# Four quads' rows of k and v loaded by SyncE instead of gathered by GpSimd, in a graph attention kernel

## The chip, the cores and the metric

The kernel runs on one core of one Trainium2 chip. A core has a matrix engine (TensorE, PE in the profile, with its weight loads as PEld), a vector engine (VectorE, DVE), a scalar engine (ScalarE, ACT), GpSimd (POOL) and SyncE (SP), which only starts transfers. SP and POOL each work off one queue of instructions in order. The transfers themselves run on 16 DMA engines. The metric is the time of one execution on the device in microseconds, the median of several runs.

## What is computed

There are 6250 nodes with 128 features each and 206250 edges, sorted by receiver. Each edge has two vectors of 32 features and a cutoff. With 8 heads of 16 features:

```python
w_ij = silu(edge_feats @ rad_W1 + rad_b1) @ rad_W2 + rad_b2
w_ij = w_ij + (silu(chi_scalar @ sph_W1 + sph_b1) @ sph_W2 + sph_b2)
q_i = (node_feats @ Wq)[receivers]          # all split into 8 heads of 16
k_j = (node_feats @ Wk)[senders]
alpha = (q_i * w_ij * k_j).sum(axis=-1) / sqrt(16) * cutoffs[:, None]
v_j = (node_feats @ Wv)[senders]
out = segment_sum(alpha[..., None] * v_j, receivers, num_segments=n_nodes) / 16
x = layernorm(x + out)
```

All is float32. What matters here: k and v belong to an edge's sender, and the senders are random nodes, so these rows have to be fetched one by one. The receivers are sorted, so q and the sums are local.

## The kernel before

**Tiles.** 128 edges make a tile, 4 tiles a quad (512 edges), 4 quads a group. There are 403 quads in 101 groups. Within a group the quads are worked in the order 0, 2, 1, 3; their places in this order are the slots 0 to 3, and `order` lists all quads in this way.

**Start.** The kernel multiplies all nodes by Wk and Wv and stores the result as a table `kv_tab` in device memory, one row of 256 numbers (1 KB) for each node: k first, then v. The senders lie in SBUF as `src_i`, one column for each tile and one partition for each edge of it.

**Loop.** For each quad, `hidden_of` (L371) puts the edge features through the first layers on PE, ACT applies silu (L396), `weigh` (L403, L405) does the second layers, `q_at_edges` (L378) brings q to the edges, `multiply` (L410) makes u = q * w on DVE, and `turn_back` (L416) turns u so that edges lie on partitions. For the quad before, `scores` (L421, L423, L424) multiplies by k and sums over each head, `messages` (L432) multiplies by v, and `sum_quads` (L442) adds messages up by receiver on PE. `statistics` (L475 to L491) makes the layernorm of a group's rows two groups later; every fourth time it writes four groups of rows.

**Rows of k and v.** `gathers(q)` issues four gathers on POOL (L114), one for each tile: each fetches 128 rows of `kv_tab` by a column of `src_i` into the tile `kv`, of which there are 16 (`RING`). They are issued 14 quads (`AHEAD`) before the quad is worked, so far as buffers and POOL allow. `kv_of[q]` names the tile that L421 and L432 read.

**Order.** All is recorded under a manual schedule: every engine works in the order in which the code names its instructions. A scheduler does not change it. So SP's queue in the loop is, for each group g: in slot 0, the load of x for g+2 (L156, with the place read from a table into a register, L118) and the load of relb (the receivers' places, as used for one-hot tables) for g+1 (L150); in slot 1, the load of edge features for g+2 (L141); in slot 2, where four groups are complete, four writes of output rows (L491, place from L118). Features and relb have two buffers each; the features' buffer is free when `hidden_of` has read the last quad of group g. DMAs from SP take turns over eight completion semaphores, and a DMA waits for the one eight before it. POOL's gathers have eight of their own.

A second, general path (L704 on) handles receivers for which the local sums don't suffice. With these inputs its loop runs zero times.

Of the kernel before, what the change touches and what calls it, by code (L numbers as in the profile page):

```python
# [13 lines left out]
F32 = mybir.dt.float32  # L14
# [7 lines left out]
SP = mybir.EngineType.SP  # L22

P = 128
N = 6250
D = 128
# [5 lines left out]
QT = 4  # L32
# [10 lines left out]
LB = 4  # L43
XQ = 8
RING = 16
CHECK = 20
NEIGHBORS = 16.0
EPS = 1e-5
# [3 lines left out]
@with_exitstack  # L52
def gnn_kernel(ctx, tc, x, src, dst, weight, edges, rad_W1, rad_b1, rad_W2, rad_b2,
               sph_W1, sph_b1, sph_W2, sph_b2, Wq, Wk, Wv, out):

# [8 lines left out]
    nc = tc.nc  # L66
# [3 lines left out]
    kv_tab = dram.tile([NB * P, 2 * D], F32, name="kv_tab")  # L70
# [6 lines left out]
    src_i = const.tile([P, NT], I32, name="src_i")  # L77
# [14 lines left out]
    gb_i = const.tile([1, NG], I32, name="gb_i")  # L92
# [17 lines left out]
    def quad_of(name, bufs, width=D):  # L110
        return ep.tile([P, QT, width], F32, name=name, bufs=bufs)
# [5 lines left out]
    def start_of(table, i, last):  # L117
        return nc.values_load(table[:1, i:i + 1], engines=(SP,), min_val=0, max_val=last,  # L118
                              skip_runtime_bounds_check_because="the table is clamped to it")
# [3 lines left out]
    order = [g * NQ + j for g in range(NG) for j in (0, 2, 1, 3) if g * NQ + j < QUADS]  # L123
    pairs = []
    for q in order:
        if q % NQ < 2:
            pairs.append([q])
        else:
            pairs[-1].append(q)
    feats_of, relb_of, act_of, kv_of, hot_of, hotT_of, x_of, q_of, msg_of = ({} for _ in range(9))  # L130
    po_of, part_of, to_of, tot_of, xT_of, y0_of, u_of, pick_of, pq_of = ({} for _ in range(9))

    def gathers(q):
        kv = quad_of("kv", RING, 2 * D)
        for t in range(QT):
            gather(kv[:, t, :], kv_tab, src_i[:, q * QT + t:q * QT + t + 1])
        kv_of[q] = kv

    def load_feats(g):
        feats_of[g] = gp.tile([P, EG // 2], F32, name="feats")  # L140
        nc.sync.dma_start(feats_of[g], edges[g])  # L141
# [4 lines left out]
    def load_rel(g):  # L146

        relb_of[g] = gp.tile([P, EQ], BF16, name="relb")
        r = rel_lin[g * GT:(g + 1) * GT, :].rearrange("(j t) e -> j (t e)", j=NQ)
        nc.sync.dma_start(relb_of[g], r[:, None, :].to_broadcast([NQ, W, EQ]))  # L150
# [180 lines left out]
    with tc.tile_pool(name="ps", bufs=1, space=PSUM) as pp:  # L331
        def pick(g):

            n = quads_in(g)
            pick_of[g] = gp.tile([P, NQ, W], F32, name="pick")
            nc.vector.tensor_tensor(
                pick_of[g][:, :n, :], colp[:, None, :W].to_broadcast([P, n, W]),
                off[:, g, :n, None].to_broadcast([P, n, W]), op=OP.is_equal)
# [110 lines left out]
        def place(g):  # L449

            to = to_of[g] = gp.tile([P, 2, P], F32, name="to")
            nc.vector.tensor_scalar(to[:, 0, :], colp, rowq[:, g:g + 1], None, op0=OP.is_equal)
            nc.vector.tensor_scalar(to[:, 1, :], colp, rowp[:, g:g + 1], None, op0=OP.is_equal)

        def part_sums(g):
            n = quads_in(g) * W
            part_of[g] = gp.tile([P, D], F32, name="part")
            nc.scalar.activation(part_of[g][:n, :], po_of[g][:n, :], AF.Copy)  # L458
# [10 lines left out]
        def statistics(g):  # L469
            first = g // LB * LB if g < NG - 2 else g  # L470
            if g == first:
                y0_of[g] = (gp.tile([P, LB, D], F32, name="y0"), gp.tile([P, LB, 2], F32, name="mv"))
            y0, mv = y0_of[first]
            k = g - first + 1
            nc.vector.tensor_tensor(y0[:, k - 1, :], tot_of[g], x_of[g], op=OP.add)  # L475
            st = gp.tile([P, 6], F32, name="st")
            nc.vector.bn_stats(st, y0[:, k - 1, :])
            nc.vector.bn_aggr(mv[:, k - 1, :], st)
            if k == LB or g >= NG - 3:
                sd = gp.tile([P, LB], F32, name="sd")  # L480
                nc.scalar.activation(sd[:, :k], mv[:, :k, 1], AF.Sqrt, bias=eps)
                rs = gp.tile([P, LB], F32, name="rs")
                nc.vector.reciprocal(rs[:, :k], sd[:, :k])
                shift = gp.tile([P, LB], F32, name="shift")
                nc.vector.scalar_tensor_tensor(shift[:, :k], mv[:, :k, 0], -1.0, rs[:, :k],
                                               op0=OP.mult, op1=OP.mult)
                for i in range(k):
                    nc.scalar.activation(y0[:, i, :], y0[:, i, :], AF.Identity,  # L488
                                         scale=rs[:, i:i + 1], bias=shift[:, i:i + 1])
                    r = start_of(gb_i, first + i, N - P)  # L490
                    nc.sync.dma_start(out[ds(r, P), :], y0[:, i, :])  # L491

        def outside(o, values, low, high):

# [13 lines left out]
        def verdict():  # L508
# [4 lines left out]
            nc.vector.tensor_reduce(found, pe[:1, :8], AX.X, OP.add)  # L513
            nc.vector.tensor_scalar(general, found, 0.0, None, op0=OP.is_gt)

        pick(0)
        turn_q(0)
        make_q(0)
# [7 lines left out]
        for g in range(NG):  # L526
            last = g == NG - 1
            for slot, j in enumerate((0, 2, 1, 3)):
                q = g * NQ + j
                i = g * NQ + slot  # L530
                if q >= QUADS:
                    continue
                if i + AHEAD < len(order):
                    gathers(order[i + AHEAD])
                if slot == 0 and 2 <= g:
                    part_sums(g - 2)
                    if g == CHECK + len(checks) + 1:
                        verdict()
                if before is not None:
                    pu = turn_back(before)  # L540
                w = weigh(q)
                if slot % 2 == 0:
                    u = 2 * g + slot // 2 + 1
                    q_and_hidden(pairs[u - 1], pairs[u] if u < len(pairs) else [])
                if slot == 1 and 2 <= g:
                    sum_group(g - 2)
                if slot == 1 and g + 1 < NG:
                    turn_q(g + 1)
                if slot == 3:
                    make_q(g + 1)  # L550
                if 1 <= g:
                    for t in ((), (0, 1), (2, 3))[slot] if last else ((), (0, 1), (2,), (3,))[slot]:
                        sum_quads(g - 1, t)
                if before is not None:
                    alpha = scores(before, pu)
                multiply(q, w)
                if before is not None:
                    messages(before, alpha)
                before = q
                if slot == 0:  # L560
                    if g + 2 < NG:
                        load_x(g + 2)
                    if g + 1 < NG:
                        pick(g + 1)
                        if 1 <= g:
                            load_rel(g + 1)
                if slot == 1:
                    if g + 2 < NG:
                        load_feats(g + 2)
                    if 1 <= g:  # L570
                        place(g - 1)
                    if last:
                        place(g)
                if slot == 2 and g + 1 < NG:
                    one_hots_T(g + 1)
                if slot == 2 and 2 <= g:
                    statistics(g - 2)
                if slot == 3:
                    one_hots(g + 1)
                    if CHECK <= g < CHECK + len(checks):  # L580
                        checks[g - CHECK]()
        g = NG - 1
# [6 lines left out]
        messages(before, scores(before, pu))  # L589
        sum_quad(g, before - g * NQ)  # L590
        statistics(g - 1)
        part_sums(g)
        sum_group(g)
        statistics(g)

    n = nc.values_load(general, min_val=0, max_val=1)
    manual.close()
# [11 lines left out]
    def general_group(g):  # L609
        with tc.tile_pool(name="lg", bufs=1) as lg, tc.tile_pool(name="lb", bufs=1) as lb, \  # L610
# [12 lines left out]
            for j in range(NQ):  # L623
                kv = lb.tile([P, QT, 2 * D], F32, name="kv_l")
                qe = lb.tile([P, QT, D], F32, name="qe_l")
                xe = lb.tile([P, QT, D], F32, name="xe_l")
# [13 lines left out]
                for i in range(2):  # L640
                    ph = pp.tile([P, EQ], F32, name="ph_l")
                    r = slice(r0 + i * R, r0 + (i + 1) * R)
# [7 lines left out]
                pw = pp.tile([P, QT, D], F32, name="pw_l")  # L650
                for t in range(QT):
                    nc.tensor.transpose(pw[:, t, :], wt[:, t * P:(t + 1) * P], ident)
                m = lb.tile([P, QT, D], F32, name="m_l")
                nc.vector.tensor_tensor(m, qe, kv[:, :, :D], op=OP.mult)
                nc.vector.tensor_tensor(m, m, pw, op=OP.mult)
                alpha = lb.tile([P, QT, HEADS], F32, name="alpha_l")
# [1 line left out]
                nc.vector.tensor_tensor(  # L658
                    alpha, alpha,
                    scale_g[:, j * QT:(j + 1) * QT, None].to_broadcast([P, QT, HEADS]), op=OP.mult)  # L660
                msg = lb.tile([P, QT, D], F32, name="msg_l")
                nc.vector.tensor_tensor(
                    msg.rearrange("p t (h e) -> p t h e", e=HD),
                    kv[:, :, D:].rearrange("p t (h e) -> p t h e", e=HD),
# [88 lines left out]
```

## Time and profile before

| | |
|---|---|
| median of 3 runs | 2914.41 us (2901.86 to 2921.47) |
| the profiled execution | 2044.89 us, span 2043.1 us |
| PE / DVE / POOL / ACT busy | 86% / 71% / 75% / 47% of the span |
| mean granted clock of PE | 0.953 |
| DMA queue of POOL: packets, MB | 76864, 209.29 |
| DMA queue of SP: packets, MB | 62912, 91.99 |

The profiled execution was much shorter than the timed runs. The profile's page lists busy time by engine, the span in slices, the DMA queues, the chain of work that ended last, and groups of instructions with their idle time before them and what ended it. Busy shares are averages: which engine sets the pace is read from who waits for whom. A line such as "L114 POOL DMA_INDIRECT kv<-kv_tab,src_i x1580" reads: line 114, engine POOL, an indirect DMA that fills kv from kv_tab by the indices src_i, 1580 times. "SPq" is SP's queue of instructions.

### The profile page before, as it was taken

To read this page: it belongs to the slowest core of one execution; us is meant where nothing else is said; L and a number is where in the kernel's file an instruction comes from. 1 tells how busy PE (TensorE), PEld (TensorE's weight loads), DVE (VectorE), ACT (ScalarE), POOL (GpSimd) and SP (SyncE) were. 2 spreads that over 40 slices of the span, in tenths; PEclk is the share of its full clock that TensorE was granted. 3 is DMA by queue.
4 is the path that set the end of the run, shared out by engine and by line. 5 is a ranking of instruction groups with operands and counts; after the bars stand their busy time and mean duration, and the time that the engine had idled before them with its cause. 6 is when DMAs were issued, how large, how long until landed. Compare 5 with 4: busy or idle time off the path is not lost.

```text
span 2043.1 us, 30097 instructions
## 1 busy us (share of the span) xinstructions
PE 1750.2 (86%) x9944; PEld 879.7 (43%) x9944; DVE 1448.5 (71%) x2976; ACT 966.7 (47%) x1826; POOL 1526.4 (75%) x1620
## 2 busy tenths in 40 slices
PE   9898889889888889788888888887888887888887
PEld 7444444444444444344444444443444443434433
DVE  6687777778676776667677676676767766767766
ACT  2545554545444445444445444444444454444443
POOL 6777777777777777777777777777777777777774
PEclk9999999999999899999999899999989999989998
DMA  8544545445445445444445454454445444544542
GB/s 304 163 150 143 154 146 156 152 133 155 148 137 156 138 144 149 148 144 144 146 141 153 134 154 142 142 154 142 144 144 150 137 152 134 153 139 145 157 138 79
DMA packets 141425, 303.66 MB, mean 149 GB/s; under 512 B 34022, under 2 KB 73808, under 8 KB 141264
## 3 DMA queue, kind: packets, MB, share of 16 engines
q0 software_dynamic: 76864, 209.29, 35.1%
q1 hardware_dynamic: 62912, 91.99, 13.7%
q8 instruction: 81, 1.33, 0.2%
q14 instruction: 80, 0.66, 0.1%
q10 hardware_dynamic: 1488, 0.40, 0.1%
HBM read 288.10 MB, written 13.46 MB: 148 GB/s over the span
## 4 chain that ended last, share of the span: by engine, by line
PE 34%; POOL 17%; DVE 16%; DMA 13%; issue 13%; ACT 6%; DVEq 0%; ACTq 0%; POOLq 0%
PE ph L403 17%; POOL kv L114 16%; DMA kv<-kv_tab,src_i 13%; PE pq L378 6%; PE pq L416 6%; DVE u L410 5%; DVE m L421 3%; PE ph L371 3%; DVE side L423 3%; ACT w L405 3%; ACT act L396 2%; DVE msg L432 2%; POOL msg L114 1%; DVE hotT L357 1%; ACT y L488 1%
## 5 line engine op out<-in xcount | busy, mean ns | idle before, releaser
L114 POOL DMA_INDIRECT kv<-kv_tab,src_i x1580 | 1494.9, 946 | 486.7 <-issue 414.0
L403 PE MATMUL ph<-act,w 128*128 128x512 f32 x1612 | 814.6, 630 | 5.0 <-ACT act L396 4.4
L405 ACT ACTIVATE w<-ph,bsum 128x512 f32<-128x512 f32 x403 | 276.5, 686 | 882.0 <-PE ph L403 879.2
L396 ACT ACTIVATE act<-ph,b 128x512 f32<-128x512 f32 x806 | 494.3, 688 | 125.6 <-PE ph L371 125.0
L416 PE MATMUL pq<-ident,u 128*128 128x128 f32 x1612 | 271.3, 293 | 239.4 <-DVE u L410 237.3
L371 PE MATMUL ph<-feats,w 32*128 32x512 f32 x1612 | 469.9, 633 | 0.0
L410 DVE TENSOR_TENSOR u<-pq,w 128x512 f32<-128x512 f32 x403 | 277.5, 688 | 269.0 <-PE ph L371 169.3
L421 DVE TENSOR_TENSOR m<-pq,kv 128x512 f32<-128x512 f32 x403 | 278.1, 690 | 225.3 <-DMA kv<-kv_tab,src_i 183.9
L403 PEld LDWEIGHTS ph<-act,w 128*128 128x128 f32 x1612 | 293.2, 203 | 223.5 <-issue 213.1
L416 PEld LDWEIGHTS pq<-ident,u 128*128 128x128 f32 x1612 | 176.7, 145 | 391.6 <-issue 218.1
L378 PE MATMUL pq<-hotT,q 32*128 32x512 f32 x806 | 291.1, 659 | 29.9 <-DVE m L421 29.4
L423 DVE TENSOR_REDUCE side<-m 128x32 f32<-128x512 f32 x403 | 280.1, 695 | 13.8
L432 DVE TENSOR_TENSOR msg<-kv,side 128x512 f32<-128x512 f32 x403 | 272.9, 677 | 0.0
L371 PEld LDWEIGHTS ph<-feats,w 32*128 32x128 f32 x1612 | 178.6, 189 | 82.3 <-issue 60.6
L378 PEld LDWEIGHTS pq<-hotT,q 32*128 32x128 f32 x806 | 81.4, 190 | 233.4 <-issue 167.8
L442 PE MATMUL po<-msg,hot 128*32 128x128 f32 x3224 | 156.2, 286 | 2.9 <-ACT part L458 2.9
L442 PEld LDWEIGHTS po<-msg,hot 128*32 128x32 f32 x3224 | 72.7, 109 | 108.3 <-issue 80.8
L424 DVE TENSOR_TENSOR side<-side,scale 128x32 f32<-128x32 f32 x403 | 80.4, 199 | 13.8
L362 DVE TENSOR_TENSOR hot<-rel,side 128x512 f32<-128x512 f32 x101 | 68.8, 681 | 0.0
L357 DVE TENSOR_TENSOR hotT<-relb,side 128x512 f32<-128x512 bf16 x101 | 68.7, 680 | 0.0
L351 PEld LDWEIGHTS ph<-wq,xT 128*128 128x128 f32 (+1 forms) x202 | 39.1, 194 | 50.4 <-issue 49.1
L463 PEld LDWEIGHTS ph<-part,to 128*128 128x128 f32 (+1 forms) x202 | 38.5, 192 | 49.3 <-issue 29.4
(85 smaller groups left out, 826.1 us busy)
## 6 DMA issues: line engine op xcount, KB each, us to landing
feats<-in_edges SPq DMA_DIRECT2D x101, 512.0 KB
kv<-kv_tab,src_i POOLq DMA_INDIRECT x1580
relb<-rel_lin SPq DMA_DIRECT2D x101, 128.0 KB
x<-in_x SPq DMA_DIRECT2D x101, 64.0 KB
out<-y SPq DMA_DIRECT2D x101, 64.0 KB
kv_tab<-kv SPq DMA_DIRECT2D x12, 512.0 KB
act<-in_x SPq DMA_DIRECT2D x12, 256.0 KB
dst_i<-in_dst SPq DMA_DIRECT2D x1, 808.0 KB
```

The lines of the kernel that those rows point to most:

```text
L114: nc.gpsimd.indirect_dma_start(out=o, out_offset=None, in_=table, in_offset=bass.IndirectOffsetOnAxis(ap=index, axis=0))
L371: nc.tensor.matmul(act_of[q, i], w1[r0:r0 + R, :], feats_of[g][r0:r0 + R, c0:c0 + EQ], start=True, stop=True)
L378: nc.tensor.matmul(pq_of[q], q_of[g][b, :], hotT_of[g][b, :], start=True, stop=True)
L396: nc.scalar.activation(act, act_of[n, i], AF.Silu, bias=b1[:, i:i + 1])
L403: nc.tensor.matmul(pw, w2[:, i, :], act_of[q, i], start=(i == 0), stop=(i == 1))
L405: nc.scalar.activation(w, pw, AF.Identity, bias=bsum)
L410: nc.vector.tensor_tensor(u_of[q], pq_of[q], w, op=OP.mult)
L416: nc.tensor.transpose(pu[:, t, :], u_of[q][:, t * P:(t + 1) * P], ident)
L421: nc.vector.tensor_tensor(m, pu, kv_of[q][:, :, :D], op=OP.mult)
L423: nc.vector.tensor_reduce(alpha, m.rearrange("p t (h e) -> p t h e", e=HD), AX.X, OP.add)
L432: nc.vector.tensor_tensor(msg_of[q].rearrange("p t (h e) -> p t h e", e=HD), kv_of[q][:, :, D:].rearrange("p t (h e) -> p t h e", e=HD), a ...
L442: nc.tensor.matmul(po_of[g][j * W:(j + 1) * W, :], hot_of[g][:, j * QT + t, :], msg_of[g * NQ + j][:, t, :], start=(t == 0), stop=(t == QT ...
```

## The change

Four quads of the 403, those at the places 98, 196, 294 and 392 of `order`, are left out by `gathers`. Their rows are loaded by SP: `load_rows(i)`, called once in each slot i, loads 128/91 rows a slot on average for the first such quad and 128/98 for the others, over the slots before it, and is done eight slots (`ROW_LEAD`) before the quad's place. Of each row p it reads the four senders of partition p into registers with one register load and issues four DMAs of one row of 1 KB each. They fill one of two new tiles `rows` (4 KB a partition each). In all there are 512 register loads and 2048 DMAs on SP.

SP's order changes in two more places. The load of relb moves from slot 0 (for g+1) to slot 1 (for g+2), behind the features. Output rows are put on a list by `statistics` and written by `write_rows` in slot 1, behind relb, and at the end of the loop. In the general path, two tiles are no longer separate but share others' space.

```diff
@@ -43,6 +43,8 @@
+ROW_QUADS = 4
+ROW_LEAD = 8
@@ -127,14 +130,37 @@
+    every = (len(order) - ROW_LEAD) // ROW_QUADS
+    row_at = [(n + 1) * every for n in range(ROW_QUADS)]
+    row_quads = {order[i] for i in row_at}
...
     def gathers(q):
+        if q in row_quads:
+            return
         kv = quad_of("kv", RING, 2 * D)
         for t in range(QT):
             gather(kv[:, t, :], kv_tab, src_i[:, q * QT + t:q * QT + t + 1])
         kv_of[q] = kv
+
+    def load_rows(i):
+
+        k = max(i + ROW_LEAD - 1, 0) // every
+        if k >= ROW_QUADS:
+            return
+        q, start = order[row_at[k]], max(k * every - ROW_LEAD + 1, 0)
+        slots = row_at[k] - ROW_LEAD + 1 - start
+        a, b = ((j * P + slots - 1) // slots for j in (i - start, i - start + 1))
+        if i == start:
+            kv_of[q] = quad_of("rows", 2, 2 * D)
+        for p in range(a, min(b, P)):
+            _, rows = nc.values_load_multi_w_load_instructions(
+                src_i[p:p + 1, q * QT:(q + 1) * QT], engines=(SP,), min_val=0, max_val=N - 1,
+                skip_runtime_bounds_check_because="senders are nodes")
+            for t in range(QT):
+                nc.sync.dma_start(kv_of[q][p:p + 1, t, :], kv_tab[ds(rows[t], 1), :])
@@ -487,8 +513,13 @@
-                    r = start_of(gb_i, first + i, N - P)
-                    nc.sync.dma_start(out[ds(r, P), :], y0[:, i, :])
+                    written.append((first + i, y0[:, i, :]))
+
+        def write_rows():
+            while written:
+                g, y = written.pop(0)
+                r = start_of(gb_i, g, N - P)
+                nc.sync.dma_start(out[ds(r, P), :], y)
@@ -562,15 +594,16 @@
                     if g + 1 < NG:
                         pick(g + 1)
-                        if 1 <= g:
-                            load_rel(g + 1)
                 if slot == 1:
                     if g + 2 < NG:
                         load_feats(g + 2)
+                        load_rel(g + 2)
+                    write_rows()
                     if 1 <= g:
                         place(g - 1)
                     if last:
                         place(g)
+                load_rows(i)
@@ -589,9 +622,11 @@
         statistics(g - 1)
+        write_rows()
         part_sums(g)
         sum_group(g)
         statistics(g)
+        write_rows()
@@ -650,7 +685,7 @@
-                m = lb.tile([P, QT, D], F32, name="m_l")
+                m = qe
@@ -658,7 +693,7 @@
-                msg = lb.tile([P, QT, D], F32, name="msg_l")
+                msg = xe
```

More of the change, by code (lines that the diff above doesn't have):

```diff
@@ L514, in verdict @@
             nc.vector.tensor_scalar(general, found, 0.0, None, op0=OP.is_gt)
+        written = []
         pick(0)
```

## The prediction, on record before the result was known

> **What bounds the kernel now.** I read the page first, for the chain that ended last and for the costliest groups (columns: line, engine, operation, tiles, count, then busy us and mean ns of one, then the idle time before them and what ended it).
>
> ```profile
> PE 34%; POOL 17%; DVE 16%; DMA 13%; issue 13%; ACT 6%; DVEq 0%; ACTq 0%; POOLq 0%
> ...
> L114 POOL DMA_INDIRECT kv<-kv_tab,src_i x1580 | 1494.9, 946 | 486.7 <-issue 414.0
> L403 PE MATMUL ph<-act,w 128*128 128x512 f32 x1612 | 814.6, 630 | 5.0 <-ACT act L396 4.4
> ...
> L421 DVE TENSOR_TENSOR m<-pq,kv 128x512 f32<-128x512 f32 x403 | 278.1, 690 | 225.3 <-DMA kv<-kv_tab,src_i 183.9
> ```
>
> The first line follows the end back: it passes through PE and POOL by turns, so no single engine stands out. PE is busiest by share (1750.2 of 2043.1 us, 86%), POOL has 75%. But POOL's idle time is 486.7 us over 1580 gathers, 0.308 us each, and nearly all is "issue": waiting for nothing. So I looked at POOL alone, in order of time, near the end:
>
> ```profile
> 2018.76 0.95 POOL L114 DMA_INDIRECT kv<-kv_tab,src_i  x1 [0.30 <-issue]
> 2020.01 0.95 POOL L114 DMA_INDIRECT kv<-kv_tab,src_i  x1 [0.30 <-DVE u L410]
> 2021.26 0.95 POOL L114 DMA_INDIRECT kv<-kv_tab,src_i  x1 [0.30 <-issue]
> 2022.51 0.95 POOL L114 DMA_INDIRECT kv<-kv_tab,src_i  x1 [0.30 <-issue]
> 2023.76 0.95 POOL L114 DMA_INDIRECT kv<-kv_tab,src_i  x1 [0.30 <-issue]
> ```
>
> A gather starts every 1.25 us, to the end. The first k-and-v gather starts at 48.8 us: 1580 x 1.25 = 1975 us, which with 48.8 gives 2024; the rest (19 us) is the last quads. POOL never waits for a buffer, and the consumer waits for POOL: the multiply m waits for a gather 115 times, 183.9 us. Four gathers make a quad, so the loop runs at 5.0 us a quad, while PE is busy 1750 / 403 = 4.3 us of it. **GpSimd's row of gathers is the bound**, with PE 0.6 us a quad behind.
>
> Last, SyncE, which gets the new work. Its own waits (us in total, times, longest):
>
> ```profile
> SPq L141 <- PE ph L371: 1214.8, 82, 21.0
> SPq L491 <- ACT y L488: 362.2, 25, 47.6
> SPq L491 <- DMA out<-y: 101.4, 75, 2.4
> ```
>
> It stands 1214.8 us before the features' buffer and 362.2 us for rows to be written: 1577 us of SP's span are free. And what a DMA with its address in a register costs SP today, from the load of x (min/median/max ns): the register load, a fused register step, a move and the DMA.
>
> ```profile
> L118 SPq TENSOR_LOAD <-gb_i x202: 263/370/788, 25.8 to 2034.7; - x101
> ```
>
> ```profile
> L156 SPq FUSED_REGOPS  x101: 37/37/56, 26.3 to 1976.4; - x101
> L156 SPq MOVE x<-in_x x101: 29/37/43, 26.4 to 1976.5; - x101
> L156 SPq DMA_DIRECT2D x<-in_x x101: 333/338/362, 26.5 to 1976.6; - x101
> ```
>
> **How this stands to the median.** The profiled execution took 2044.9 us (span 2043.1), the three timed runs 2902 to 2921, median 2914.4: 870 us more, which no view explains. If POOL is the bound there too, a gather costs (2914.4 - 69.9) / 1580 = 1.80 us, with 69.9 = 2044.9 - 1975 for start and end. That POOL holds the end in both is my choice: it is the engine without slack in the trace.
>
> [...] 0.946 us of POOL for a gather, 0.34 us of SP for a load of 512 KB. [...] Here one register from SBUF takes 370 ns in the middle; four at once are not in this trace.
>
> **The change, part by part.**
> 1. Removed from POOL: 4 quads x 4 = 16 of 1580 gathers. At 1.25 us that is 20.0 us of the profiled execution; at 1.80 us it is 28.8 us of the median. Is it all won? After each skipped quad POOL is one quad ahead, and the consumer must catch up at the 5.0 - 4.3 = 0.7 us a quad that PE leaves at most. Skips lie 98 quads apart, and 10 quads follow the last (position 392 of 403): 7 us against the 5.0 to win. So nearly all; from below 18 us in the profile. From above, a row quad lies in SBUF eight quads early and so has no wait for a landing: those waits are 183.9 / 115 = 1.6 us, at most 4 x 1.6 = 6.4 us more. I take a third, 2 us.
> 2. Added to SP: 512 rows, each a load of four registers and four times (fused register step, move, DMA). One such step from the rows above: 0.037 + 0.037 + 0.338 and gaps of about 0.1, so 0.5 us. A row is 0.37 + 4 x 0.5 = 2.4 us if four registers cost what one does, and 4 x 0.37 + 2.0 = 3.5 us if each is fetched for itself[...]. I take 2.4 to 3.0. Then 512 rows are 1230 to 1540 us, and SP has 1577 free in the profiled execution and 1577 + 870 = 2447 in the median. Break-even is 1577 / 512 = 3.08 us a row, or 4.78 us. What hides the part is SP's wait for the features' buffer; without it, features, relb and x come late.
> 3. Queued behind a row on SP: features of g+2, relb, x, outputs. Features become free to load about slot 0 of group g and are used in slot 2 of g+1, more than four quads (20 us) later; SP's rows between are at most two a slot, 6 us. Nothing is late while the sum holds. The row DMAs take turns over the same eight completion semaphores as SP's other DMAs, so a row waits for the DMA eight before it, about 4 us old: nothing, if a 1 KB row lands in that time, and SP loses the excess if not.
> 4. The load of relb goes from slot 0 of g for g+1 to slot 1 of g for g+2: three quads earlier for the use. DVE's wait for relb is not among the waits now, so 0 either way. Its 0.57 us of SP is only moved.
> 5. Outputs are recorded and written at slot 1 of the next group, past features and relb in SP's row. That takes away the 362.2 us wait before ACT's y, which would have held rows behind it; nothing but the end waits for an output, and at the end they are written where they were. The waits of one output for the one before (101.4 us) stay. Cost 0; if an output's buffer came free late, ACT would wait, but there are two buffers of four groups.
> 6. Traffic: 2048 packets of 1 KB in place of the same bytes by gathers. [...] A delay in landing hits m directly, since the gathers come just in time, but it shifts the end only once, not per gather: below 2 us. The two product tiles that share other buffers are in the general path, which does not run.
>
> Sum: profiled execution 2044.9 - 20 - 1 = about 2024; median 2914.4 - 28.8 - 2 = **2883 us**, -1.1%.
>
> **Rivals.**
> - *SP becomes the bound* (slower). Mechanism: SP's in-order row; place: the features' load, whose wait for PE vanishes and turns into PE's wait for features. It decides from 3.08 us a row at the profile's pace, 4.78 us at the median's. At 3.5 us rows cost 1792 us, 215 more than free: profiled execution 2260 us, +10%. In the median it would need SP stretched like the whole (2914 / 2045 = 1.43), then about 3220 us; with SP at its profiled speed it would not show. For it: no margin at four separate fetches. Against: 870 us more room in the timed runs.
> - *POOL is not the bound of the timed runs*, and the 870 us belong to PE or a common brake: gain 0, 2914 us. For it: PE is at 86%; against: POOL's unbroken row.
> - *Row loads disturb the gathers* (does not do what it says): [...] 0.04 us more per gather would eat 1580 x 0.04 = 63 us: about 2945. The trace of before can't exclude it; its DMA engines are busy less than half.
>
> **How the numbers follow.** A measurement of this kernel tells about 1% from no change. Gain as summed 0.70: the sum lies near that bound, so 0.54 beyond and 0.16 within. POOL not the bound 0.05, within. SP the bound 0.20, slower; disturbance 0.05, slower. So faster 0.54, same 0.21, slower 0.25. The gain case alone spans 2862 (5 us of part 1's upper side and the runs' spread of 10) to 2896 (gather at 1.25 us: 2894). The range reaches to mild disturbance and a slightly overfull SP: 2862 to 2990; a fully bound SP is left out.
>
> **What would show it.** Right: 1564 gathers still 1.25 us apart, span near 2023, m's waits for kv slightly less, SP still waiting for PE's ph before features, 100 to 350 us in sum. A row's cost is read between two register loads. Wrong: features or x as releasers of PE, SP's wait for PE gone (SP bound); gathers further apart than 1.25 us (disturbance); gathers fewer but the time unchanged (other bound).

## The result, and the profile after

The changed kernel takes 2955.72 us (median of 6, 2932.88 to 2961.95), the kernel before 2911.9 us in the same comparison (2901.86 to 2921.47). The ratio is 1.0159, 95% interval 1.0121 to 1.0196: **1.6% slower**, where 1.1% faster was forecast. Here and below, medians are of all runs and ratios of fast runs alone (those within 1.5% of the fastest), so a ratio can differ from that of the medians, by up to 0.7%.

The page of the changed kernel shows another picture than the page that the prediction was read from. Its chain of waits and three of its groups:

```profile
PE 36%; another core or an unknown queue 22%; DVE 14%; issue 13%; ACT 7%; POOL 5%; DMA 1%; SPq 0%; DVEq 0%; ACTq 0%; POOLq 0%
...
L117 POOL DMA_INDIRECT kv<-kv_tab,src_i x1564 | 1478.5, 945 | 1342.2 <-DVE msg L458 809.9
...
L431 ACT ACTIVATE w<-ph,bsum 128x512 f32<-128x512 f32 x403 | 276.7, 687 | 1268.6 <-PE ph L429 496.2
L447 DVE TENSOR_TENSOR m<-pq,kv 128x512 f32<-128x512 f32 x399 | 275.4, 690 | 752.4 <-remote 546.0
```

A gather still takes 945 ns. But POOL now waits 809.9 us for buffers that DVE frees (msg), and DVE waits 546.0 us for a "remote" releaser, one that the records don't name (in the chain "another core or an unknown queue", though the kernel runs on one core). As POOL stands before full buffers, the gathers are ahead of DVE. Is that the change's doing? The kernel before, run again (b0_before), answers:

```profile
PE 42%; another core or an unknown queue 24%; DVE 16%; issue 9%; ACT 6%; POOL 2%; DMA 1%; DVEq 0%; SPq 0%; ACTq 0%; POOLq 0%
...
L114 POOL DMA_INDIRECT kv<-kv_tab,src_i x1580 | 1493.7, 945 | 1229.0 <-DVE msg L432 738.6
...
L405 ACT ACTIVATE w<-ph,bsum 128x512 f32<-128x512 f32 x403 | 276.6, 686 | 1315.7 <-PE ph L403 662.8
L421 DVE TENSOR_TENSOR m<-pq,kv 128x512 f32<-128x512 f32 x403 | 278.2, 690 | 706.4 <-remote 560.5
```

It isn't. The same kernel, unchanged, has a span of 2847.4 us here and the same waits. The page shown before, with 2043.1 us and no wait of POOL for a buffer, is of another regime than every timed run shown with it. The program runs in one of two ways, and all runs made together go the same way: near 2045 us on one of the five chips in my experiments, and near 2870 to 2905 us on the other four, like the runs of the comparison above. I put that down to the chip; but each chip was used on one occasion only, so chip and occasion can't be told apart.

**What differs between the chips** is seen best at one place of the timeline. Here it is for the kernel with deferred outputs (e5_outs): start and length in us, engine, line, operation; in brackets the idle time before and its releaser. First DVE:

```profile
1358.15 0.34 DVE L453 TENSOR_SCALAR to<-side,rowp 128x128 f32<-128x128 f32 x1
1367.18 0.69 DVE L421 TENSOR_TENSOR m<-pq,kv 128x512 f32<-128x512 f32 x1 [8.69 <-remote]
```

Then PE in the same stretch:

```profile
1357.77 0.38 PE L416 MATMUL pq<-ident,u 128*128 128x128 f32 x2
1357.99 1.88 PE L403 MATMUL ph<-act,w 128*128 128x512 f32 x4
...
1360.34 0.59 PE L371 MATMUL ph<-feats,w 32*128 32x512 f32 x1
1367.93 1.21 PE L378 MATMUL pq<-hotT,q 32*128 32x512 f32 x1 [7.00 <-DVE m L421]
```

ACT, and then POOL:

```profile
1361.41 0.28 ACT L345 ACTIVATE xT<-ph 128x128 f32<-128x128 f32 x1 [1.14 <-issue]
1367.24 0.69 ACT L405 ACTIVATE w<-ph,bsum 128x512 f32<-128x512 f32 x1 [5.56 <-remote]
```

```profile
1362.53 0.94 POOL L114 DMA_INDIRECT kv<-kv_tab,src_i  x1 [0.30 <-issue]
1363.78 0.95 POOL L114 DMA_INDIRECT kv<-kv_tab,src_i  x1 [0.30 <-issue]
1370.29 0.94 POOL L114 DMA_INDIRECT kv<-kv_tab,src_i  x1 [5.56 <-DVE msg L432]
```

By its records PE has turned u back (L416) at 1358.15, yet DVE, which needs only that and rows that were gathered quads ago, starts m at 1367.18. ACT, idle since xT ended at 1361.69, starts w in the same instant (1367.24), though its matmuls (L403) end at 1359.87. Both signals come from PE, and they come 9 and 7 us late; meanwhile POOL gathers on until its buffers are full. I call this a **hold**. It comes about once a group: a w is over 4 us late 91 times in the 101 groups of the changed kernel. Summed over the 403 quads, w starts 666 us after the end of its matmuls in b0_before and 684 us in the changed kernel, against 72 us in the page shown before. The difference, 594 us, is most of the 804 us by which the span of b0_before is longer. Ends of matmuls are modelled, so the trace can't tell whether PE stands still or only its signals are late.

The low clock belongs to it: 0.819 in b0_before and 0.808 after, against 0.953. In the trace of the changed kernel the granted clocks are 1.0 and 0.5 alone, in steps of 3.41 us, and in 94 of its 115 gaps of PE over 2.5 us a half-speed spell begins within the gap, 3.1 us after the gap's start at the median. So in those 94 the half clock follows the gap and isn't what brings it about.

### The profile page after: what moved, and what is told of

It reads as the page before. It is cut to its first block, busy times and chain, and to the rows that moved or that the text cites. A ratio compares the mean times of both kernels' runs of the same rounds, so it can differ in the third digit from the quotient of the medians.

```text
span 2956.3 us, 36907 instructions
## 1 busy us (share of the span) xinstructions
PE 2102.9 (71%) x9944; PEld 1004.2 (34%) x9944; DVE 1451.8 (49%) x2976; ACT 987.4 (33%) x1826; POOL 1509.8 (51%) x1604
## 4 chain that ended last, share of the span: by engine, by line
PE 36%; another core or an unknown queue 22%; DVE 14%; issue 13%; ACT 7%; POOL 5%; DMA 1%; SPq 0%; DVEq 0%; ACTq 0%; POOLq 0%
PE ph L429 15%; PE pq L404 7%; PE pq L442 6%; POOL kv L117 5%; PE ph L397 5%; DVE u L436 3%; ACT w L431 3%; DVE m L447 3%; ACT act L422 3%; DVE msg L458 3%; DVE side L449 2%; PE po L468 1%; PE pk L243 1%; DMA kv<-kv_tab,src_i 1%
## 5 line engine op out<-in xcount | busy, mean ns | idle before, releaser
L117 POOL DMA_INDIRECT kv<-kv_tab,src_i x1564 | 1478.5, 945 | 1342.2 <-DVE msg L458 809.9
L429 PE MATMUL ph<-act,w 128*128 128x512 f32 x1612 | 947.8, 719 | 13.6 <-ACT act L422 13.2
L447 DVE TENSOR_TENSOR m<-pq,kv 128x512 f32<-128x512 f32 x399 | 275.4, 690 | 752.4 <-remote 546.0
L397 PE MATMUL ph<-feats,w 32*128 32x512 f32 x1612 | 609.5, 743 | 22.2 <-ACT w L431 11.2
L404 PE MATMUL pq<-hotT,q 32*128 32x512 f32 x806 | 374.7, 737 | 325.2 <-DVE m L447 322.7
L442 PE MATMUL pq<-ident,u 128*128 128x128 f32 x1612 | 309.4, 323 | 385.5 <-DVE u L436 323.4
L429 PEld LDWEIGHTS ph<-act,w 128*128 128x128 f32 x1612 | 339.1, 233 | 283.9 <-issue 261.4
L442 PEld LDWEIGHTS pq<-ident,u 128*128 128x128 f32 x1612 | 201.1, 161 | 550.0 <-issue 327.3
L404 PEld LDWEIGHTS pq<-hotT,q 32*128 32x128 f32 x806 | 100.8, 217 | 568.9 <-DVE m L447 377.0
L397 PEld LDWEIGHTS ph<-feats,w 32*128 32x128 f32 x1612 | 208.9, 221 | 151.0 <-issue 78.4
L493 ACT ACTIVATE tot<-ph 128x128 f32<-128x128 f32 x101 | 27.7, 274 | 188.9 <-PE ph L397 124.9
```

Of the source, the lines that this page charges most:

```text
L117: nc.gpsimd.indirect_dma_start(out=o, out_offset=None, in_=table, in_offset=bass.IndirectOffsetOnAxis(ap=index, axis=0))
L397: nc.tensor.matmul(act_of[q, i], w1[r0:r0 + R, :], feats_of[g][r0:r0 + R, c0:c0 + EQ], start=True, stop=True)
L404: nc.tensor.matmul(pq_of[q], q_of[g][b, :], hotT_of[g][b, :], start=True, stop=True)
L429: nc.tensor.matmul(pw, w2[:, i, :], act_of[q, i], start=(i == 0), stop=(i == 1))
L442: nc.tensor.transpose(pu[:, t, :], u_of[q][:, t * P:(t + 1) * P], ident)
L447: nc.vector.tensor_tensor(m, pu, kv_of[q][:, :, :D], op=OP.mult)
```

## The experiments

Ratios are to the kernel before on the same chip, with 95% intervals. Kernels measured together ran on one chip, and what is compared is mostly taken from such a set.

### First set: order or rows? (chip held, before 2874.43 us)

**b0_before**: the kernel before, unchanged.

> The kernel before, unchanged, to see with a profile what holds its timed runs. Theory A (the timed runs are in a state in which POOL isn't the bound: consumers start late behind PE): about 2912 us, granted clock near 0.81, POOL waits for DVE's msg (buffers) for several hundred us, m does not wait for gathers. Theory B (POOL is the bound in timed runs too, only slower): 2912 us with gathers about 1.8 us apart and no wait of POOL for a buffer.

Measured: 2883.31 us, 0.9976 (0.9930 to 1.0022). Its page is the one above.

**e1_order**: SP's new order alone, all quads gathered.

```diff
-    row_quads = {order[i] for i in row_at}
+    row_quads = set()
...
-                load_rows(i)
```

> The new order on SP alone (relb a group earlier, output rows one slot later), all quads gathered, no row loads. Theory A1 (the row loads on SP cost the 45 us): 2912 us within 10. Theory A2 (the moved relb and outputs cost it): 2950 to 2960 us.

Measured: 2962.28 us, 1.0271 (1.0189 to 1.0353).

**e2_bulk**: the changed kernel with a single load of 512 KB for each of the four quads instead of 512 rows; the senders' own rows of these quads are left out.

```diff
-        for p in range(a, min(b, P)):
...
+            nc.sync.dma_start(kv_of[q], kv_tab[:EQ, :].rearrange("(p n) d -> p n d", p=P))
```

> The four quads are not gathered; in each slot SP loads 512 consecutive rows of the table into the quad's tile in one DMA instead of the senders' rows (which are left out), so that POOL is relieved without 2048 small DMAs, with one 512 KB load per slot as traffic. Theory A1 (small row loads cost): 2912 us within 15, as the 16 gathers are worth nothing here. Theory B (POOL is the bound): 2885 us. If removing gathers itself costs: 2950.

The load is made once for each of the four quads, not in each slot as the expectation has it.

Measured: 2959.22 us, 1.0258 (1.0176 to 1.0340).

**e3_both**: all quads gathered, and the 2048 row loads into tiles that nobody reads.

```diff
-        if q in row_quads:
-            return
...
-            kv_of[q] = quad_of("rows", 2, 2 * D)
+            spare_of[q] = quad_of("rows", 2, 2 * D)
...
-                nc.sync.dma_start(kv_of[q][p:p + 1, t, :], kv_tab[ds(rows[t], 1), :])
+                nc.sync.dma_start(spare_of[q][p:p + 1, t, :], kv_tab[ds(rows[t], 1), :])
```

> All quads gathered as before, and the 2048 row loads made beside them into tiles that nothing reads. Theory A1: 2950 to 2965 us, as after. Theory B (gathers' removal would win 29 us but rows cost 73): about 2985 us. If the quads' own data path costs: 2912 us.

Measured: 2957.8 us, 1.0246 (1.0159 to 1.0333).

The order alone costs no less here than the whole change did in its own comparison. With that order, 2048 row loads more (e3 against e1) and 16 gathers fewer (e2 against e1) both change nothing beyond the intervals of 0.8%.

### Second set: which edit of the order? (chip held, before 2904.57 us)

**e4_relb**: relb's load moved alone.

```diff
-                        if 1 <= g:
-                            load_rel(g + 1)
...
                         load_feats(g + 2)
+                        load_rel(g + 2)
```

> The kernel before with one edit: the load of the receivers' places (relb) moved from slot 0, for the group after, to slot 1, for the group after that, directly behind the features' load. Outputs are issued where they were. Theory P (two loads of the group issued next to each other are what costs): the whole loss of the order, ratio 1.02 to 1.03 to before, about 2960 us against 2880. Theory O (the deferred outputs cost): ratio 1.00, about 2880. Theory H (each half costs): about 1.013, 2915. My prediction's own step (cost 0) is the middle case for this edit alone.

Measured: 2887.19 us, 0.9943 (0.9914 to 0.9971).

**e5_outs**: the outputs deferred alone.

```diff
-                    r = start_of(gb_i, first + i, N - P)
-                    nc.sync.dma_start(out[ds(r, P), :], y0[:, i, :])
+                    written.append((first + i, y0[:, i, :]))
...
                         load_feats(g + 2)
+                    write_rows()
```

> The kernel before with one edit: the outputs' DMAs are issued in slot 1 instead of directly behind the activation that makes them; relb is loaded where it was. Theory P: ratio 1.00, about 2880 us. Theory O: 1.02 to 1.03, about 2960. Theory H: about 1.013, 2915.

Measured: 2995.65 us, 1.0316 (1.0248 to 1.0384). Theory O holds: of the two edits it is the outputs' deferral, which I had costed at nothing.

**e6_norelb** and **e7_nofeats**: does a load of SP bring the holds about?

```diff
     def load_rel(g):
+        if g > 1:
+            relb_of[g] = relb_of[g - 2]
+            return
...
     def load_feats(g):
+        if g > 1:
+            feats_of[g] = feats_of[g - 2]
+            return
```

The first edit is e6, where the receivers' places (relb) of all groups but two are left out, the second e7, where the features are.

> The kernel before with relb loaded for groups 0 and 1 alone and used again by all later groups: the receivers' places of the later groups are left out. Theory S-relb (the stall of some 7 us once a group, in which the signals of TensorE come late, belongs to the broadcast load of relb): the stalls go, about 2050 to 2200 us at a clock near 0.95. Theory S-feats (it belongs to the features' load): about 2880 us. Theory S-none (it belongs to neither): about 2880 us.

> The kernel before with the features loaded for groups 0 and 1 alone and used again by all later groups: the features of the later groups are left out. Theory S-feats: the stalls of some 7 us once a group go, about 2050 to 2200 us at a clock near 0.95. Theory S-relb: about 2880 us. Theory S-none: about 2880 us.

Measured: 2869.92 us, 0.9886 (0.9786 to 0.9985), and 2878.43 us, 0.9907 (0.9876 to 0.9938). The lateness of w still sums to 650 and 673 us. S-none: neither load makes the holds.

### Third set: where outputs leave, and POOL (chip not held, before 2045.15 us)

**e8_outs0**: outputs behind x and relb but ahead of the features.

```diff
                             load_rel(g + 1)
+                    write_rows()
```

> The kernel before with one edit: the outputs are issued in slot 0 of the next group, behind the loads of x and relb and ahead of the features' load, so x and relb no longer stand behind SP's wait for y, while the outputs still leave as soon as y is there. Theory W (SP's wait for y, which holds x and relb back in one group of four, is what keeps the groups from falling into one pattern): as e5_outs, ratio 1.02 to 1.03, every group 28 to 29 us. Theory T (it is the time at which the outputs leave, 23 to 29 us into the group instead of 3 to 13): as before, ratio 0.99 to 1.00, with one group in four near 25 us.

Measured: 2044.6 us, 0.9996 (0.9987 to 1.0005). On a chip without holds this can't decide between W and T.

**e9_rows**: the changed kernel with the outputs issued in place again.

```diff
-                    written.append((first + i, y0[:, i, :]))
+                    r = start_of(gb_i, first + i, N - P)
+                    nc.sync.dma_start(out[ds(r, P), :], y0[:, i, :])
...
-                    write_rows()
```

> The changed kernel with one edit undone: the outputs are issued again directly behind the activation that makes them; the four quads still come by rows and relb is loaded in slot 1. If the deferral is the whole loss and the row loads cost nothing: ratio 0.98 to 1.00, about 2870 us. If rows that stand behind SP's wait for y come late and hold the messages of their quads: 1.01 to 1.03, about 2940.

Measured: 2029.97 us, 0.9924 (0.9908 to 0.9941). The expected number had the held regime in mind; but here the prediction's sum can be checked at last. From its page, then the gathers of before and of this kernel (min/median/max ns, first and last start in us), then SP's waits:

```profile
L117 POOL DMA_INDIRECT kv<-kv_tab,src_i x1564 | 1479.6, 946 | 479.0 <-issue 405.3
```

```profile
L114 POOL DMA_INDIRECT kv<-kv_tab,src_i x1580: 942/946/1282, 48.8 to 2023.8; - x198
```

```profile
L117 POOL DMA_INDIRECT kv<-kv_tab,src_i x1564: 942/946/1439, 46.8 to 2001.7; - x196
```

```profile
SPq L517 <- ACT y L514: 177.3, 24, 43.2
SPq L167 <- PE ph L397: 133.8, 41, 17.8
```

POOL again waits for nothing (405.3 us of "issue", 0.3 each), and its gathers are still 1.25 us apart. The last one starts 22.0 us earlier, 2.0 of them because the first one does. But from the last gather to the end it takes 26.2 us where it took 19.4, so the span is only 15.2 us shorter: part of the gain is lost in the last quads. Why isn't shown. The waits give the rows' price: features' buffer 1214.8 to 133.8, y 362.2 to 177.3, in sum 1266 us of SP filled by 512 rows, 2.47 us a row. The row's own instructions (count, then min/median/max ns):

```profile
L159 SPq TENSOR_LOAD <-src_i x512: 295/567/907, 61.6 to 1913.8; - x171
```

```profile
L163 SPq FUSED_REGOPS  x2048: 37/37/43, 62.0 to 1915.7; - x187
L163 SPq MOVE rows<-kv_tab x2048: 29/29/38, 62.5 to 1915.7; - x187
L163 SPq DMA_DIRECT2D rows<-kv_tab x2048: 224/228/314, 62.6 to 1915.8; - x187
```

Four registers cost 567 ns, not four times 370; a row's DMA 228 ns, not 338.

**e10_half**: every odd quad but the first eight uses the rows of the quad before it; its own senders' rows are left out.

```diff
     def gathers(q):
+        if q % 2 and q > 8:
+            kv_of[q] = kv_of[q - 1]
+            return
```

> The kernel before with half of the gathers: every odd quad but the first eight uses the rows of the quad before it again, its own senders' rows are left out. My prediction's choice (POOL's gathers hold the end of the timed runs too, 1.80 us each): some 780 gathers fewer, a fall of up to 1400 us, until TensorE binds at about 1800 us. Theory A (TensorE with its held signals and its half clock binds, POOL waits for its buffers): 2850 to 2890 us, ratio 0.99 to 1.00.

Measured: 1891.15 us, 0.9243 (0.9224 to 0.9261). The chain of work that ended last has no POOL left:

```profile
PE 57%; DVE 24%; ACT 13%; issue 5%; DMA 1%; ACTq 0%; SPq 0%; DVEq 0%
```

So without holds POOL is the bound, and PE is next, 154 us behind.

**e11_lb2**: outputs normalized and written for two groups at a time.

```diff
-LB = 4
+LB = 2
```

> The kernel before with outputs normalized and written for two groups at a time instead of four (LB = 2): 25 more square roots and their small DVE steps, outputs leave in every second group. Theory T or W (a group with outputs in it is followed by one of 25.3 us instead of 27 to 29): two groups in four are short, 2 to 3 us fewer for 25 groups more, about 2820 us, ratio 0.975 to 0.985. If the short group has nothing to do with the outputs: 1.00 to 1.01.

Measured: 2043.55 us, 0.9993 (0.9986 to 0.9999). It would have spoken only on a held chip; inconclusive.

### Fourth set: the same questions on a held chip (before 2896.84 us)

**e12_after**: the change as it is.

> The changed kernel as it is. Theory A (two regimes): on a chip where TensorE is held once a group (the kernel before near 2880 us) ratio 1.012 to 1.030; on one where it isn't (before near 2045 us) the 16 gathers that are taken from POOL count: ratio 0.985 to 0.995, about 2030 us. Theory B (the deferred outputs cost on every chip): 1.01 to 1.03 on both.

Measured: 2943.53 us, 1.0171 (1.0083 to 1.0260).

**e13_rows**: the kernel of e9_rows.

> The changed kernel with the outputs issued directly behind the activation again. Where TensorE is held: if the deferral is the whole loss, ratio 0.985 to 1.000 and 2 to 3% under the changed kernel; if rows that wait behind SP's wait for y are late, 1.01 to 1.03. Where it isn't: 0.992 again.

Measured: 2951.82 us, 1.0215 (1.0148 to 1.0281). Putting the outputs back doesn't win the loss back. That the deferral is the whole loss has fallen.

**e14_outs0**: the kernel of e8_outs0. 

> The kernel before with the outputs issued in slot 0 of the next group, behind x and relb and ahead of the features. Where TensorE is held: theory W (SP's wait for y that holds x and relb back is what breaks the pattern) 1.02 to 1.03; theory T (the time at which the outputs leave) 0.99 to 1.00. Where it isn't: 1.00 again.

Measured: 2958.07 us, 1.0234 (1.0167 to 1.0300). The outputs leave when they did before (25.5 us after the first w of their group in the middle, 25.4 in b0_before), and only x and relb no longer stand behind them; the loss is there. That is theory W's range, not T's. But which of the two loads it is stays open: e4 took relb alone out from behind the wait and lost nothing, and x alone was not tried. SP waits for y as long as before, in b0_before and then here:

```profile
SPq L491 <- ACT y L488: 451.6, 23, 43.0
```

```profile
SPq L496 <- ACT y L488: 449.6, 25, 42.7
```

What the losing kernels share shows in the length of a group, from the first w of one to the first w of the next. Means in us over groups 5 to 95, by place in the four that write outputs together (outputs are ready late in place 1):

| kernel | 0 | 1 | 2 | 3 | all |
|---|---|---|---|---|---|
| b0_before | 27.8 | 28.9 | 25.3 | 27.2 | 27.3 |
| e4_relb | 28.1 | 29.4 | 25.2 | 27.8 | 27.6 |
| e5_outs | 29.1 | 29.1 | 28.7 | 28.7 | 28.9 |
| e14_outs0 | 28.4 | 28.8 | 28.2 | 28.3 | 28.4 |
| e13_rows | 28.1 | 28.7 | 28.1 | 27.6 | 28.1 |
| e12_after | 28.1 | 28.9 | 28.2 | 27.3 | 28.1 |

The kernel before has one short group in four, right behind the outputs. Every kernel that loses has lost it. In e5 and e14 the w of a group that is most late starts 15.2 to 16.0 us after its first w in 87 and 85 of the 91 groups, as if the loop had fallen into step with the holds; in b0_before in 40. That isn't shown for the change as a whole: in e12 it is 57, in e13 43. 101 groups at 28.4 instead of 27.3 are 111 us; the spans of e14 and b0, on two chips, differ by 101.

**e15_half**: the kernel of e10_half.

> The kernel before with half of the gathers (every odd quad but the first eight uses the rows of the quad before again, its own are left out). Where TensorE is held: if POOL holds part of the end, as my prediction chose, a fall by more than 100 us (ratio under 0.96); theory A: 0.98 to 1.01. Where it isn't: 0.924 again.

Measured: 2203.66 us, 0.7621 (0.7550 to 0.7691), 693 us less. Theory A as I had put it, TensorE alone and gathers irrelevant, has fallen. Most of the time in holds is gone: a w is over 4 us late once, where it was 84 times in b0_before, though still over 1 us late about once a group (98 times).

```profile
L114 POOL DMA_INDIRECT kv<-kv_tab,src_i x792 | 751.0, 948 | 1247.3 <-DVE msg L435 988.7
...
L424 DVE TENSOR_TENSOR m<-pq,kv 128x512 f32<-128x512 f32 x403 | 275.5, 684 | 231.2 <-PE ph L374 128.1
```

POOL stands still even longer, for buffers; DVE's waits before m are 231.2 us instead of 706.4; the lateness of w sums to 203 us. PE is busy 82% of the span instead of 71%, so a busier PE doesn't by itself bring holds.

### Fifth set: gathers or bytes? (chip held, before 2868.69 us)

**e16_bf16**: the same gathers, half the bytes; k and v are rounded to bf16.

```diff
-    kv_tab = dram.tile([NB * P, 2 * D], F32, name="kv_tab")
+    kv_tab = dram.tile([NB * P, 2 * D], BF16, name="kv_tab")
```

> The kernel before with k and v rounded to bf16 in the table and in the tiles, so that each of the same gathers moves half the bytes. Where TensorE is held (before near 2880 us): theory bytes, 2100 to 2400 us (ratio 0.73 to 0.83); theory gathers (the number of gathers or scattered rows counts, not their bytes), 2800 to 2890 (0.97 to 1.00). Where it isn't held (before near 2045): 1.25 us a gather as before, ratio 0.98 to 1.00.

**e17_halfbulk**: half of the gathers, the same bytes; odd quads but the first eight take the first 512 rows of the table in one load, and their senders' rows are left out.

```diff
+        if q % 2 and q > 8:
+            nc.sync.dma_start(kv, kv_tab[:EQ, :].rearrange("(p n) d -> p n d", p=P))
```

> The kernel before with half of the gathers: every odd quad but the first eight takes one load of 512 KB, the first 512 rows of the table, by SyncE into its own tile; its senders' rows are left out. Where TensorE is held: theory bytes, 2750 to 2890 us (ratio 0.95 to 1.00); theory gathers, near e15_half, 2200 us (0.76 to 0.80). Where it isn't held: near e10_half, 0.92 to 0.95.

Measured: 2904.67 us, 1.0199 (1.0091 to 1.0307), and 2277.48 us, 0.7973 (0.7878 to 0.8068). POOL's queue on the two pages, e16 first:

```profile
q0 software_dynamic: 51584, 105.75, 13.1%
```

```profile
q0 software_dynamic: 39040, 105.96, 16.0%
```

Both move the same bytes by gather, and SP makes up the rest in e17 (195.28 MB on its queue instead of 91.99). The lateness of w sums to 665 us in e16 and 298 us in e17. The time in holds goes with the number of gathers (or of what comes with each: rows fetched, completions, records of them), not with bytes.

## Why the prediction was wrong

**The step that failed** is the choice after "870 us more, which no view explains": "That POOL holds the end in both is my choice". On the chip of the profile POOL does hold the end. On the chips of the timed runs it waits over 700 us for buffers, and holds set the pace. What was forecast as a gain of 28.8 us is nothing that can be measured there (e2 against e1), and the loss comes from a term put at nothing, the outputs of part 5. Stretching a gather from 1.25 to 1.80 us spread over POOL what happens at PE's signals. The rival "POOL is not the bound of the timed runs ... a common brake" was the right one; it got 0.05 and a gain of 0, with no case in which a brake makes the loop sensitive to SP's order.

- *Part 1, the gathers.* Right in mechanism on the unheld chip: 20 + 1 us predicted there, 15.2 us measured with outputs in place, under the 18 us that the prediction gave as the lower side. POOL's own 20 us came; the last quads after it took 6.8 us longer, against the reckoning that the consumers catch up. The full change was not run on such a chip. On a held one, e15 gives 693 / 788 = 0.88 us a gather on average, 14 us for 16, which is 0.5% and inside the scatter of e2 against e1.
- *Part 2, the rows.* Right: 2.4 to 3.0 us a row predicted, about 2.47 found, and SP not full. In part by luck, since a dearer register load (567 ns for 370) and a cheaper DMA (228 for 338) offset each other; and the upper end of 3.0, between the 2.4 and 3.5 worked out from the trace, was a choice that no measurement showed.
- *Part 3.* Right without holds. With holds and outputs in place, rows aren't free: e13 (relb moved and rows) stands at 1.0215, e4 (relb moved alone) at 0.9943, though on two chips.
- *Part 4, relb.* Cost 0: e4 is even 0.6% faster.
- *Part 5, outputs.* "Cost 0" is the term of the sum that cost most: alone it is 3.2%. I reasoned that only the end waits for an output. But the edit also takes SP's wait for y away from in front of x and relb, and e14, which does only that, costs 2.3% on a held chip. It isn't the only way to lose: e13 has the outputs, and with them x behind the wait, where they were, and loses 2.1%.
- *Part 6 and "Row loads disturb the gathers".* e3 against e1 shows no such cost. Rows did go whole, as the prediction took it: SP's queue in the changed kernel has 4096 packets more than before, two for each of the 2048 rows, one of the row's 1 KB and one of 4 bytes, so no row was spread over the 16 engines. Which engine took them isn't in the trace. The queue's packets, MB and share of the engines' time:

```profile
q1 hardware_dynamic: 67008, 94.09, 9.9%
```

**What is settled.** On a held chip the new order of SP suffices for the loss, and in it the deferral; row loads behind outputs in place lose as much; the parts don't add up, as each takes away the same short group. **What stays open**: why SP's standing before y makes the next group short, and what a hold is. On the latter one lead, which was not tried: for the same kernel the trace of the unheld page keeps 38780 records of semaphore updates, that of b0_before 16903. That holds and records go together is my guess. With half of the gathers there are fewer records, 26635 in the page of e10_half, as there is less time in holds (203 us of lateness of w in e15 where b0_before has 666). But a plain count doesn't fit: the page of e9_rows, with its row loads, has 42927, 4147 more than before, which in proportion to the 12145 and the 693 us of half the gathers would be some 240 us; e3 against e1 shows nothing of it. And every run here carries records, so there is no time without them, and no run shows the connection.

No version beats the kernel before by more than 1% on a held chip with the computation whole; e4_relb, at 0.9943, is the nearest.

## What to carry to other kernels

When the profiled execution and the timed runs differ by 40% (2044.89 and 2914.41 us), the profile shows another course of the program than the one that is timed: get one whose span fits the timed runs before costing anything, and until then let neither the bound nor a duration be stretched to fit. Where a recurring stall sets the pace, an edit that is free by every sum can still change how the loop meets the stall (e5_outs: 3.2% slower), so an in-order queue's waits are to be tested by themselves, one edit at a time. And removing a little of something (16 gathers, e2 against e1) can show nothing where removing half of it shows the largest effect of all (693 us, e15).

## What was unexpected of the hardware

- The same program took 2045 us on one chip and 2869 to 2905 us on four others, each used on one occasion.
- On those four, PE's signals come late about once a group (27 to 29 us): w starts 650 to 673 us after its matmuls, summed over the 101 groups of b0_before, e6, e7 and e16 (three of the four chips), which is 6 to 7 us a group. With half of the gathers the time falls by 24% (e15), with half of their bytes not at all (e16, 1.0199).
- Without holds a transfer of one 1 KB row takes SP 228 ns, and a load of four registers from SBUF 567 ns, where one register took 370.
